# A four-layer graph network on one core: the first batch's adjacency transposed by TensorE, and the order tables written anew with another rule for the port that VectorE and GpSimd share

## The chip, the cores and the metric

One core of a Trainium2 chip runs the whole program. The core has five engines with an instruction queue each: TensorE (PE in the profile, with its weight loads as PEld), VectorE (DVE), ScalarE (ACT), GpSimd (POOL) and SyncE (SP). The metric is the device time of one execution in microseconds (us). The time of a kernel is the median of several executions. One more execution is recorded by the profiler, and its span runs from the first to the last instruction.

## The reference

There are 32 batches of 512 nodes with 128 features (x), and one 512 x 512 matrix of zeros and ones for each batch (adj, about 3% ones). Four layers follow each other, all of the form x + f(relu(layernorm(x)), adj):

```
layer 0:  p = h @ (W1 - W2);  q = h @ W2;  f[n] = max over m of relu(p[n] + q[m] + b) * adj[n, m]
layer 1:  four times: f = tanh([ norm(adj) @ src | self | norm(adj)^T @ dst ] @ wu + bu)
layer 2:  f = (adj / rowsum(adj)) @ (h @ w) + bias
layer 3:  four times a GRU cell on m = adj^T @ (h @ w3[l])
```

Both adj and its transpose are used in every batch. Layer 0 is a maximum over neighbours. It can't be one matrix product, and it is where most of the work on VectorE lies.

## The kernel before

The batches are independent, and the kernel works on several of them at a time. `batch(b)` is written once and has five parts. `load` fetches x and adj. `prepare` computes the normalised features, the transposed adjacency `at`, the products p and q (`pn`, `qn`, a table of q in memory), running counts of neighbours (`pc`, `cc`, `ccd`) and the indices of up to seven neighbours that are left over (`pkey`, `top`, `at8`, `idx`). `gathers` forms the maximum of layer 0 in two ways. For the first four neighbours of each column block, VectorE or ScalarE builds a selection matrix `oh` from `ccd`, TensorE multiplies it (`pa`), and VectorE takes the maximum into `acc`. The neighbours left over are fetched by GpSimd's indirect DMAs into `G`, and VectorE takes the maximum into `gm`. `layer1` and `layer23` do the rest; their products with the adjacency (`pg`) use each operand as a rounded part `hi` and a remainder `lo`. GpSimd computes `lo` with a subtraction in `sbuf_parts` (three times a batch), ScalarE computes `hi`.

In `prepare`, the transposed adjacency is made like this. ScalarE reads each of the four row blocks of the float32 matrix `af` and writes a bf16 copy `ab`, while it adds up the row sums. SyncE then issues four DMA transposes of 2-byte data from `ab` to `abt`. ScalarE copies `abt` to `at`, while it adds up the column sums. `ab` has two buffers and `abt` has one, which the next batch's `junk` also uses (a check that the matrix holds only zeros and ones).

**What sets the order.** Calls do not issue instructions. `Flow` records them with the buffers that they read and write, and then orders them. Every recorded operation has a due time in a table (`FRONT`, `MIDDLE`, `BACK`), and on every engine the operations stand in the order of these due times. `Flow.step` goes through the five queues with a simple model of the engines, in which every operation has a cost, and the model only decides in what order the queues take buffers and banks, and where TensorE is given `spin` matmuls (products of constants, into an unused bank, that keep it busy while it would wait). All instructions that go through `Flow` have one line in the profile, L1107; `spin` has L1133. `FRONT` has 12 rows: three for the weights and nine for batches 0 to 8. `MIDDLE` is one row, used for 13 batches, each shifted by `PERIOD`. `BACK` has ten rows, for batches 22 to 31. So from batch 9 to 21 the engines repeat one order.

**The port in the planner.** VectorE and GpSimd share a port to the on-chip memory. `Engine.note` marks the operations that take it (`port`): those with two large inputs in that memory, VectorE's `tensor_scalar`, and some on GpSimd. In `Flow.starts`, a marked operation of one engine starts only after the marked operation of the other. If GpSimd asks (`asked`) while VectorE holds the port and VectorE's next operation is marked too, the planner of this kernel lets VectorE go on: that is what `held` says.

Of the kernel before, what the change touches and what calls it, by code (L numbers as in the profile page):

```python
# [15 lines left out]
BF16 = mybir.dt.bfloat16  # L16
# [5 lines left out]
AX = mybir.AxisListType  # L22
# [20 lines left out]
    546.48,  # L43
    (
        "!!!!+b!+#!*D!*m!+u!4.!4?!4F!3o!Ab!KY!ZS![x!zp!|3!{=!{g!lw!^@!gV##n#(]#[`#_Z#_f#`C#dm!oU!"
        "v-#&f#)i#f%#fr#gc#hS#j6#n~#qX#th#oM#lm#pB#q{#tF#sb#u8#va#r*#ng#o9#pX#rV#ox#s7#p{#qI#x*$*"
        "7#u:$)V#qd#vg$#p#~r#wI$(v#sf#}R$%s$#3$!R#~5#m)#p|#rn$(~$8P$;:$=,#JN#x)#x7#}7#}>#~:$!%#x0"
        "#x>#yK#yQ#ym#zX#yX#{a#{}#|>#|c#}N#|i#})#}0$&k$,N$.P$/;$k^$/h$?n$A|$J_$1{$3A$6*$;[$0X$<B$"
        "4d$?[$7L$C2$9q$Io$?k$IF$A1$IZ$EX$Q1$JK$T>$Kn$U4$N2$Vn$Qj$^r$U($_*$VJ$_{$Wo$e<$_N$gX$aQ$k"
        "e$bt$ky$f%$ph$h5$p|$lA$u8$md%!v$qD$~9$t5%!M$uq$~M#{C#|P#~($$_$&`#|$$*Q$-/$,$$1O$!m$.=$3%"  # L50
        "$1w$45$)R$33$65$6Q$6}$4r$6j$8L$:l$>3$5S$;&$>{$?4$?q$:e$?K$A3$A.$D($@Q$DM$Dy$EN$Ez$BP$E}$"
        "G<$F~$H($CF$I.$Jg$MF$P;$FZ$N#$Rr$OS$S^$He$][$^5$]t$_>$TR$^:$b`$`~$cK$UH$a9$d7$bi$f2$a~$d"
        ";$j|$fT$l1$eQ$k=$nc$p~$sl$v0$y{$z1${0%#V%$G%%m%)K%(.%&k$RE%*9$`R%)=%(]$k$%Gq%H/%0e%0X%1b"
        "%-8%1M%4^%92%1v%5I%;l%<(%;s%=5%?=%=I%>?%=r%?x%Ao%OW%IR%KH%Mm%N2%NP%I^%J1%Jv%L&%L>%LU%Ll%"
        "MU%O0%Iv%JH%J_%KS%M&%Pa%Qx%S4%Sy%Q2%WA%X;%Y6%ZD%[=%[R%]$%]E%]e%^S%_R%`$%a=%aT%al%c>%cm%d"
        "(%dZ%`<%`k%a%%b>%bU%bm%c&%dV%eX%cU%dn%f8%g3%hA%i@%iK%iV%ix%j:%jy%kO%lh%m!%mQ%qH%qa%qx%rI"
        "%su%kh%l!%l9%mi%n;%nR%o$%r2%s8%n#%oS%pM%ra%t&%u6%v1%w?%xE%xP%y~%{V%{u%|W&$>&$U&&)&&@&(W&"
        "(o&)*&*+&,E&$m&%V&%n&&n&()&(@&)A&)X&-c&%?&03&3Q&5G&6q&7l&8f&9a&=s&Bl&Cz&Dy&E(&E2&E=&E]&H"
        "+&KY&H|&KE&LU&L]&MX&LN&N@&NX&O)&Of&Qe&Oz&RZ&R1&S5&TI&_M&YT&Z<&ZS&Zk&[%&[=&]&&]U&cr&eu&fY"
        "&gL&gn&iE&k^&hD&kx&j$&lg&mE&l{&l7&ml&me&m>&m~&n:&nK&oG&qO&pY&q&&o[&v;&w&&ts&u)&u4&uF&uf&"  # L60
        "vn&wt&xo&y*&yL&yd&y{&z6&zM&ze&{4&|2&}3&}@&~b(!S&{7&~.&~-(!Q(#>(#7($/(&1((-((8((C((N((m()"
        "O((Y()T(*N(*g(*~(+P(+h(+~(,9(,h(-7(.u(0B(0&(1P(2B(-!(27(1&(3F(42(5u(5#(6b(8F(9$(9:(9E(:?"
        "(;1(9P(:c(<X(>&(>>(>U(?&(?U(?m(@((@S(C4(AQ(DB(D~(F3(<p(D.(E/(F*(Fs(F{(Gd(HO(IN(IY(Ip(I{("
        "JX(KJ(J)(K#(K{(LM(L|(M7(Mf(M}(N8(NO(Nz(Ox(Ps(QU(Rt(Sf(N~(Qn(RB(S4(S}(TH(U)(Ur(Vz(W4(Wb(W"
        "m(Xl(Yg(XQ(Z$(ZK"
# [6 lines left out]
            "!!M!!!!*t!+,!*`!+8!+x!&r!0q"  # L72
# [13 lines left out]
        6.86,  # L86
        (
            "!%S!%&![B!jS!il!j=!i=!jr!!!!jq!ia!j2!n6!-:!j_!jH!j{!l+!ls!ml!m1!yV!vi!z<!zw!k>!ym!z&!y@!"
            "zP!{<!|w!zz#+`#,<#-z#.W!~)#,2#-o#,&#.1#.z#1>#/I#@M#@y#@c#C*#.y#@X#A(#@n#AG#B3#EU!#}#DB#F"
            "i"  # L90
# [5 lines left out]
            "!!!!$!!!O!)^!)5!)q!)I!*7!*0!*>!*)!*P!*i!*X!+v!-N!-%!,.!/m!1)!/-!09!;O!=H!.2!.G!.^!0O!0y!"  # L96
            "4G!6]!<R!>E!Fn!G_!HO!Iu!1p!4b!7e!5p!3g!2k!8*!8L!8W!9<!<0!=&!8W!Gn!IC!Jc!M&!J%!LF!H^!L*!W"
            "N!]L!Md![l!Jc!MO!Vn!V1!SR!Zq!Km!S@!X/!UP!Tp!T3!Jk!K0!N(!N;!NO!Nd!d5!>>!Ls!M(!Mn!N.!Ot!Q3"
            "!Mg!Mu!M|!N&!NA!O-!Q:!QH!QO!QV!Rg!T%!QA!Q^!Qe!Qk!R*!UT!V}!Zr!W7!Rx!Sq![Q!`H!c1!YO!ak!_%!"
            "e{!dU!hd!u=!j*!gA!qC!rf!|B!kL!w4!un!xX#%^!y{!~i!}F!|##+r##/#/r#.O#-,#8W#$Q#(T#+f#&2#9C!T"  # L100
            "m!Uh!V7!V#!W@!V@!W;!X-!WS!Xu!T%!W(!Ye!Z4!Y}!Z}!Y@!]!!^M!bs!^f!c_!eI!fE!fq!f]!g]!f+!g%!hH"
            "!il!j;!f+!gG!j&!k&!j>!ko!i9!jT!l!!l[!l:!qO!m^!qg!r;!rC!s(!n?!rZ!sp!s6!t[!np!u=!vh!x0!w!!"
            "yM!vY!wu!yC!zu!yb!{a!uz!yx!}!!z3!}k!wN!zJ#!,!{3##T!yX!zt!|B#$@!}z#&>!|f!~%#$3#(]#&C#*I#+"
            ">#+e#+p#+{#:b#<##>+#>J#=h#=I#>|!Wp!^&!]F!XP#3d#3~!gN#A6#A^#AJ#Ar#B*#B8#B1#B?#C(#De#EM#I*"
            "#M1#J1#I=#JZ#Ni#Q(#:q#Mq#M|#N*#N5#OB#O_#Rg#Rt#S0#S=#SI#Sb#So#UL#P%#RZ#S##SU#S{#T+#T7#TD#"
            "Ts#P3#TP#Ti#Tv#U%#U2#U?#UK#Uz#P?#T]#UW#Ud#Uq#U}#V-#V^#V}#VP#We#Vj#XA#W9#Wr#XT#Xm#Y<#Y|#Z"
            "##Z/#ZZ#Zf#ZM#Zx#[)#[|#[*#[W#[e#[q#[}#]`#]l#^A#_7#[=#].#]:#]R#]x#^(#^5#^Y#_X#[I#^M#^g#^s"
            "#_0#_<#_T#_b#`$#]F#_!#_H#_n#_z#`*#`7#`C#`d#`O#b&#`[#b:#a,#aW#b:#bg#c6#cu#cb#d(#dW#dc#dG#"
            "e3#eP#f6#d~#e|#f,#fE#g&#g?#h:#k=#k^#e5#eo#f8#f^#fj#fw#g3#gL#i9#eH#gX#gp#g}#h-#hF#hl#if#l"
            "E#fQ#hR#h_#i(#i4#iA#iM#iY#l##hx#kQ#is#ko#jB#l|#jn#n-#lP#o)#mL#nX#o<#oT#p##pc#q-#q8#qC#rR"  # L110
            "#q^#r+#rq#sb#r9#s*#s=#sb#tB#t[#u<#v7#x!#rE#sI#sU#so#s{#th#tt#un#y%#tN#u##uH#uU#ub#u{#v+#"
            "v]#z&#vC#vP#vi#vu#w%#wB#wO#wr#{E#x=#|p#xI#}{#xu#~c#yO$!2#y{$!^#zJ$#E#zv$#q#{^$$@#|-#|}#~"
            "_$$l$%R$&X$&i$&t$(8$([$)g$0K$//$/B$/V$1G$0`$3h$2|$5;$5S$5W$7{$8]$83$9R$9)$:-$<,$AC$:~$=j"
            "$>$$><$>S$>k$?%$@+$Bw$EW$F)$F?$FU$I?$Gt$IY$It$K8$KL$L]$Ka$M&$Lq$L|$LU$MA$MY$M:$Pi$Rj$Qt$"
            "P}$R@$S`$TX$TZ$Vi$W!$W.$W]$XS$YX$ZS$Zw$[2$[I$[x$]3$]J$]b$^0$_&$_~$`5$a0$b$$]y$aK$a!$bY$c"
            "F$cO$dD$eb$fa$gg$gr$g}$h?$i]$fl$hC$i>$jh$k#$k;$kR$kj$l#$l;$lg$me$pO$ns$q_$s2$lj$qJ$pt$sp"
            "$t]$v?$u_$w,$x.$x9$y>$yI$yh$zK$xC$yY${N${g$|9$|g$|~$}9$}P$~!$~N%%*%#G%&8%$U%([%!L%&R%(8%"
            ")3%)|%*(%*m%+v%,k%,v%-#%-/%-W%.c%-:%.M%/G%/`%/w%0I%0a%0w%12%1I%1u%2l%4y%46%6+%7/%1a%5t%6"
            "N%7@%8-%8e%9E%:c%;W%;c%<*%<4%<v%=N%=i%=4%>3"
# [3 lines left out]
        4.19,  # L123
        (
            "!!!!:U!0)!0Q!0=!/r!0x!0q!1*!1!!1<!1T!2O!2h!=f!=<!AG!;<!G{!Hu!LK!Tw!WY!T(!T3!T=!TH!Zg!LV!"
            "My!Uh!YF!ab!do!g|!if![^!^j!iU!`Y!]C!^>!aA!`{#$(##D#$w#&C!j&!cV!h`!q6!rS!qs!s4!en!i5!~D#("
            "Q!{v##B!lB!u@!|V!}7#!b#!$!lq#$i#16#0U#/@#.`!k.!p&!tQ!w<!wP!we!wx!XO!md!sS!sb!sw!ze!|%!sZ"
            "!si!sp!s~!u*!vG!zz!{,!{:!{H!~:#)L#&b#&i#&p#&w#(l#+`#+U#2Q#/G#(C#.&#.E#<v#><#?z#B<#08#EJ#"
            "2x#G(#5E#Hf#6o#LI#F4#Nc#IB#QQ#L=#TG#Ns#V}#P9#XZ#R.#Z<#U##^/#X-#a8#YQ#cR#Zu#dR#^g#fr#aq#i"
            "|#dF#lP#ei#n-#g[#of#jW#s=#m-#ub#nf#wB#pB#xM#sv#|v##8#(N#(z#(f#*u#*7#-O#-{#-g#.g#*p#,t#.B"  # L130
            "#/R#.e#0?#.7#/w#1E#1q#2X#3(#6>#79#8=#7Q#9*#7[#8W#9r#8o#;:#2F#4_#9*#<%#9A#<o#5{#8F#:##@*#"
            ":m#@r#>`#?[#BN#@-#C=#?H#A]#Dc#B/#FG#;%#>U#B^#G=#C0#H)#@9#B[#En#I$#F*#L^#D$#Fg#Nw#Le#Oc#E"
            "_#MX#PN#RR#T[#G@#It#V$#Xo#VR#Y[#L1#Mq#`*#`W#`S#ao#c~#g~#hX#j<#}l#~p$#<$$=$#z$#Z$%##1<#3|"
            "#9_#1y$$7$$Q#x0$&q$&^$&I$()$(=$(R$(D$(K$):$+`$)A$,m$-w$-#$.C$-M$.z$/f$*#$.Y$.e$/&$/1$/S$"
            "/o$1k$2U$2m$3>$4($4?$4V$5,$0B$2&$3U$3m$4n$5)$5@$5W$6%$0Y$0q$6A$7S$8b$9V$9b$9m$9x$:O$;2$;"
            "V$<s$=.$=E$>F$?/$?F$?^$@-$;n$<-$<[$=]$>]$>t$@p$AY$C<$>/$?u$C@$D=$EK$F@$FR$Fe$Fp$GO$H2$H@"
            "$Is$J]$MB$MZ$Mr$N-$O>$Ot$H_$I-$ID$I[$JE$Jt$L)$PQ$P}$J.$K.$LH$ND$OV$Q!$R,$S:$T;$TF$Ug$W)$"
            "WG$ZV$]6$^`$_2$`b$aK$ac$b5$bc$cW$^w$_I$_a$_x$`3$a4$az$bL$bw$`y$f*$jy$n_$oq$pl$q~$s4$vm$z"
# [2281 lines left out]
```

## Time and profile before

| | |
|---|---|
| time, three executions | 2809.97, 2811.62, 2818.3 us; median 2811.62 |
| profiled execution | 2811.83 us, span 2810.1 us |
| TensorE busy | 2715.8 us, 97% of the span |
| VectorE busy | 2450.8 us, 87% |
| GpSimd busy | 1687.4 us, 60% |
| ScalarE busy | 1263.9 us, 45% |
| mean granted TensorE clock | 0.993 |

The profiled execution is 0.2 us from the median, and 1.7 us longer than its span. A matmul counts as busy from its start until its modelled end, and the next one can start long before that, so 97% doesn't say that TensorE never waited. Times in the trace are counted from the start of the span. Two things give the pace. The store of a batch's result (`out_dram<-xo`, on ScalarE's queue) is the last instruction of a batch, so the distance of two stores is the time that one batch takes in the pipeline; the first is at 280.28 us and the last at 2799.9 us. The windows of the first 320 us show how the pipeline fills.

### The profile page before, as it was taken

Reading aid. Unit: us, or ns where it says so; the run is one execution under the profiler, and the core shown is the slowest. Engines: PE = TensorE matmul, PEld = TensorE weight load, DVE = VectorE, ACT = ScalarE, POOL = GpSimd, SP = SyncE. Lnnn points to the kernel's source line nnn. Section 1 sums busy time; section 2 is a strip of 40 time slices with the busy share of each in tenths; the row PEclk is TensorE's granted clock in tenths of the full one; section 3 lists DMA queues with packets and bytes.
Section 4 is the critical chain, followed back from the end, with each engine's and each line's share of the span. In section 5 each row is a group of like instructions: output and inputs, shape, how many; then the busy total and the mean of one; then the engine's idle time right before and its main releaser. Section 6 shows DMA issues by size and latency. Waiting matters only on the chain.

```text
span 2810.1 us, 36215 instructions
## 1 busy us (share of the span) xinstructions
PE 2715.8 (97%) x10690; PEld 1719.9 (61%) x10690; DVE 2450.8 (87%) x5739; ACT 1263.9 (45%) x2623; POOL 1687.4 (60%) x1892
## 2 busy tenths in 40 slices
PE   7799999999999999999999999999999999999997
PEld 4475666666666665666666666666666565656575
DVE  5888988899999998999999999999999898988544
ACT  5744444444444443444444444444444444443333
POOL 3766666666666666666666666666666666665410
PEclk9999999999999999999999999999999999999999
DMA  7754544344445444444444444454444454333200
GB/s 168 127 97 78 90 92 88 67 83 85 97 94 98 86 70 76 90 93 98 91 67 89 83 91 94 98 91 70 87 83 90 91 93 93 62 64 61 40 5 9
DMA packets 256752, 233.81 MB, mean 83 GB/s; under 512 B 98426, under 2 KB 205092, under 8 KB 256548
## 3 DMA queue, kind: packets, MB, share of 16 engines
q0 software_dynamic: 47104, 92.34, 24.4%
q1 hardware_dynamic: 143172, 81.41, 12.3%
q10 hardware_dynamic: 66272, 57.68, 6.9%
q8 instruction: 87, 1.43, 0.2%
q14 instruction: 117, 0.96, 0.1%
HBM read 163.79 MB, written 17.17 MB: 64 GB/s over the span
## 4 chain that ended last, share of the span: by engine, by line
PE 62%; DVE 21%; issue 7%; ACT 4%; POOL 4%; DMA 2%; SPq 0%; ACTq 0%; DVEq 0%; POOLq 0%
PE pg L1107 19%; PE pu L1107 13%; PE pk L1107 11%; DVE acc L1107 5%; PE pa L1107 4%; PE phn L1107 3%; DVE nn L1107 3%; PE pxn L1107 2%; DVE oh L1107 2%; DVE gm L1107 2%; PE ph L1107 2%; DVE h L1107 2%; ACT xn L1107 2%; DVE gate L1107 2%; PE pq L1107 1%
## 5 line engine op out<-in xcount | busy, mean ns | idle before, releaser
L1107 POOL DMA_INDIRECT G<-qtab,idx x744 | 786.5, 1057 | 530.3 <-DVE gm L1107 324.8
L1107 DVE TENSOR_TENSOR acc<-acc,pa 128x512 f32<-128x512 f32 x992 | 672.9, 678 | 43.2 <-PE pa L1107 14.0
L1107 PE MATMUL pa<-oh,qhl 128*128 128x512 f32 x1024 | 469.5, 488 | 18.6 <-DVE acc L1107 8.4
L1107 PE MATMUL pg<-an,hi 128*128 128x512 f32 (+1 forms) x1072 | 453.0, 429 | 0.2 <-ACT hi L1107 0.2
L1107 PE MATMUL pu<-ag,w 128*128 128x512 f32 (+1 forms) x952 | 440.8, 570 | 2.1 <-DVE ag L1107 2.1
L1107 PE MATMUL pg<-an,lo 128*128 128x512 f32 (+1 forms) x1072 | 411.6, 393 | 1.8 <-DVE lo L1107 1.0
L1107 DVE TENSOR_SCALAR oh<-ccd 128x1024 fp32r<-128x1024 bf16 x492 | 341.4, 705 | 3.1 <-PE pa L1107 2.9
L1107 ACT ACTIVATE xn<-x,shift,rstd 128x128 f32<-128x128 f32 x512 | 217.7, 485 | 233.4 <-POOL shift L1107 214.4
L1107 PE MATMUL pg<-at,hi 128*128 128x512 f32 (+1 forms) x672 | 284.1, 432 | 2.6 <-ACT hi L1107 1.9
L1107 PEld LDWEIGHTS pa<-oh,qhl 128*128 128x128 f32 x1024 | 191.5, 192 | 129.1 <-issue 57.6
L1107 PE MATMUL pg<-at,lo 128*128 128x512 f32 (+1 forms) x672 | 260.5, 396 | 0.6 <-POOL lo L1107 0.6
L1107 PEld LDWEIGHTS pu<-ag,w 128*128 128x128 f32 x952 | 174.3, 190 | 132.6 <-issue 100.1
L1107 PE MATMUL pk<-mT,g_ih 128*128 128x512 f32 (+1 forms) x528 | 254.5, 583 | 0.7 <-ACT mT L1107 0.7
L1107 PE MATMUL pk<-h,g_hh 128*128 128x512 f32 (+1 forms) x528 | 251.3, 582 | 0.9 <-ACT h L1107 0.7
L1107 PEld LDWEIGHTS pg<-an,hi 128*128 128x128 f32 x1072 | 201.8, 188 | 77.3 <-issue 22.8
L1107 ACT ACTIVATE gate<-pk,bsum 128x512 f32<-128x512 f32 (+1 forms) x264 | 173.0, 670 | 160.3 <-PE pk L1107 119.8
L1107 PEld LDWEIGHTS pg<-an,lo 128*128 128x128 f32 x1072 | 201.8, 188 | 69.9 <-issue 21.0
L1107 DVE TENSOR_TENSOR gm<-gm,G 128x128 f32<-128x128 f32 x744 | 232.8, 328 | 7.5 <-DMA G<-qtab,idx 6.5
L1107 ACT COPY mT<-pg 128x512 f32<-128x512 f32 (+1 forms) x164 | 93.9, 572 | 311.0 <-PE pg L1107 274.0
L1107 POOL TENSOR_TENSOR lo<-xn,hi 128x512 fp32r<-128x512 f32 x96 | 130.9, 1363 | 120.7 <-ACT hi L1107 116.4
L1107 POOL TENSOR_TENSOR rstd<-rstd,mhalf 128x4 f32<-128x4 f32 x128 | 139.9, 1093 | 102.1 <-DVE shift L1107 50.4
L1107 DVE TENSOR_TENSOR ag<-pg,rbc 128x512 f32<-128x512 f32 (+1 forms) x272 | 173.4, 650 | 20.6 <-PE pg L1107 18.9
(178 smaller groups left out, 5117.7 us busy)
## 6 DMA issues: line engine op xcount, KB each, us to landing
ccd<-cc SPq DMA_DIRECT2D x512, 64.0 KB
an<-in_adj_dram POOLq DMA_DIRECT2D x128, 256.0 KB
af<-in_adj_dram ACTq DMA_DIRECT2D x31, 1024.0 KB
rbc<-scal SPq DMA_DIRECT2D x32, 512.0 KB
x<-in_x_dram ACTq DMA_DIRECT2D x62, 256.0 KB
G<-qtab,idx POOLq DMA_INDIRECT x744
qtab<-qn SPq DMA_DIRECT2D x32, 256.0 KB
out_dram<-xo ACTq DMA_DIRECT2D x32, 256.0 KB
```

The source lines that it names most:

```text
L1107: op.fn(*(real(v) for v in op.args), **{k: real(v) for k, v in op.kw.items()})
```

## The change

There are three edits.

The first is in `prepare`, for batch 0 alone. The four DMA transposes and the buffer `abt` go. TensorE transposes the 16 blocks of 128 x 128 from `af` (float32) into four banks `pat`, and ScalarE copies these to `at` with the same instruction as before, which now reads a bank. The bf16 copies `ab` of batch 0 are still made, since their instruction adds up the row sums.

```diff
-        abt = F.tile(big, [P, NT, NT, P], BF16, tag="abt", name=f"abt_{b}")
-        for it in range(NT):
-            F.sync.dma_start_transpose(out=abt[:, it, :, :], in_=abs_[it])
+        if b:
+            abt = F.tile(big, [P, NT, NT, P], BF16, tag="abt", name=f"abt_{b}")
+            for it in range(NT):
+                F.sync.dma_start_transpose(out=abt[:, it, :, :], in_=abs_[it])
         for jt in range(NT):
+            if b:
+                v = abt[:, :, jt, :]
+            else:
+                v = pst(0, f"pat_{b}_{jt}")
+                for it in range(NT):
+                    F.tr(v[:, it, :], af[:, it, jt * P : (jt + 1) * P], W.ident, v)
             F.act.activation(
-                at[:, jt, :].rearrange("p (i q) -> p i q", q=P), abt[:, :, jt, :], AF.Identity,
+                at[:, jt, :].rearrange("p (i q) -> p i q", q=P), v, AF.Identity,
                 accum_out=deg[:, 1, jt : jt + 1],
             )
```

The second is the planner's rule for the port. When GpSimd asks between two marked operations of VectorE, or while the first of them runs, the port now goes to GpSimd at the end of that first one, and VectorE's next marked operation starts after GpSimd's.

```diff
                 asked = max(self.free["pool"] - self.HOLD, ops["pool"].ready)
-                held = self.port["vec"] > asked and self.port["vec"] > self.free["pool"]
-                if not held and asked < at["vec"] <= at["pool"] <= at["vec"] + self.HOLD + 1e-9:
-                    at["vec"] = at["pool"] + 1e-6
+                got = max(at["pool"], self.port["vec"])
+                if asked < at["vec"] <= got <= at["vec"] + self.HOLD + 1e-9:
+                    at["vec"] = got + 1e-6
```

The third is the tables: all of `FRONT`, `MIDDLE` and `BACK` have other due times. `FRONT` now has ten rows (batches 0 to 6), `BACK` nine (23 to 31), and `MIDDLE` serves the 16 batches 7 to 22. `PERIOD` and every cost of the planner stay. Every operation of a batch other than the first is the same as before; what differs is the order on all five engines, the buffers and banks that follow from it, and the number of `spin` matmuls (181 before, 165 after).

```diff
 MIDDLE = (
-    546.48,
+    369.07,
...
 FRONT = (
...
-    2161.25,
+    2233.47,
...
```

In a batch of the repeated order the instructions around GpSimd's subtraction `lo` of layer 1 stood like this before, and stand like this after (numbers of batches left out; both columns are orders, not times):

```
        VectorE                                            GpSimd
before  acc, lo(layer 3), oh, gm, oh, acc, acc, acc        gather, gather, lo, gather, rstd, has
after   oh, lo(layer 3), gm, oh, acc, acc, oh, acc         gather, an, has, lo, rstd, gather
```

In the first batch SyncE's queue before held the four transposes among the loads of the weights, ahead of the copies `ccd<-cc`. Afterwards these copies stand directly behind the loads of the bias rows, and the loads of `wn`, `wd` and `ws` of later weight groups stand among and behind them.

## The prediction

> **What bounds the kernel now.** I read the page's head first, then windows of one batch each in the repeated part, then the instructions of VectorE, GpSimd and the weight loads around the longest VectorE instruction in them, and last the first 50 us.
>
> ```profile
> span 2810.1 us, 36215 instructions
> ...
> PE 2715.8 (97%) x10690; PEld 1719.9 (61%) x10690; DVE 2450.8 (87%) x5739; ACT 1263.9 (45%) x2623; POOL 1687.4 (60%) x1892
> ...
> L1107 DVE TENSOR_TENSOR gm<-gm,G 128x128 f32<-128x128 f32 x744 | 232.8, 328 | 7.5 <-DMA G<-qtab,idx 6.5
> ```
>
> TensorE and VectorE are both close to full, so a wait on either can reach the other. The third line is odd. The groups by tile give the same 744 instructions as 247/282/1558 ns (shortest, median, longest). The mean of 328 is 46 ns above the median, 744 x 0.046 = 34 us in all: a few are very long.
>
> The windows from one store of a result to the next, and one such long instruction (VectorE, GpSimd, weight loads of TensorE; start, length, and in brackets the idle time before and what ended it):
>
> ```profile
> 1610.31:1692.29 81.98, 81.53 (x317) 51.62 (x315) 76.60 (x179) 37.23 (x78) 52.48 (x59) 1.00 0.46 88
> 1692.29:1774.25 81.96, 81.51 (x317) 51.60 (x315) 76.58 (x179) 37.21 (x78) 52.54 (x59) 1.00 0.45 88
> ```
> ```profile
> 1663.60 0.68 DVE L1107 TENSOR_SCALAR oh<-ccd 128x1024 fp32r<-128x1024 bf16 x1
> 1664.20 1.36 DVE L1107 TENSOR_TENSOR gm<-gm,G 128x128 f32<-128x128 f32 x1
> 1665.48 0.68 DVE L1107 TENSOR_SCALAR oh<-ccd 128x1024 fp32r<-128x1024 bf16 x1
> ...
> 1663.73 1.69 POOL L1107 TENSOR_TENSOR lo<-xn,hi 128x512 fp32r<-128x512 f32 x1 [0.42 <-issue]
> ...
> 1666.81 0.19 PEld L1107 LDWEIGHTS pa<-oh,qhl 128*128 128x128 f32 x1 [0.69 <-DVE acc L1107]
> ...
> 1676.54 0.20 PEld L1107 LDWEIGHTS ph<-ident,h 128*128 128x128 f32 x2 [0.54 <-DVE h L1107]
> ```
>
> A batch takes 81.97 us (DVE is the third busy column). In it GpSimd's `lo` starts at 1663.73, while VectorE runs `oh`. VectorE's next instruction, `gm`, takes 1.36 instead of 0.28, and ends when `lo` has ended; `lo` takes 1.69 where its median is 1.28. So the port went to GpSimd between two instructions of VectorE, and VectorE stood for 1.08 us. The planner of before says that VectorE goes on in this place. After it VectorE has no idle time until 1683, and TensorE waits for it twice.
>
> The start (the last line is the first selection matrix of layer 0):
>
> ```profile
> 11.29 2.28 DVE L1107 SCALAR_TENSOR_TENSOR junk<-af 128x2048 bf16<-128x2048 f32 x1
> ...
> 16.40 1.32 SPq L1107 DMA_TRANSPOSE abt<-ab  x1
> ...
> 23.28 1.20 SPq L1107 DMA_TRANSPOSE abt<-ab  x1
> ...
> 31.22 0.63 ACT L1107 ACTIVATE at<-abt 128x512 fp32r<-128x512 bf16 x1
> ...
> 34.94 0.64 ACT L1107 ACTIVATE at<-abt 128x512 fp32r<-128x512 bf16 x1
> ...
> 44.28 0.66 DVE L1107 TENSOR_SCALAR oh<-ccd 128x1024 fp32r<-128x1024 bf16 x1
> ```
>
> All of `af` is there at 11.29, since `junk` reads it whole, but the first piece of `at` is copied at 31.22. The 20 us between go to copies, two buffers `ab` that wait for each other, four transposes on SyncE's queue and their landing.
>
> **The change part by part.** *The regular stall.* Read one by one, `gm` takes 1.36 at one place in each of the 20 batches 7 to 26 (first at 591.7, last at 2156.7 us). In the new order `lo` is followed on VectorE by two `acc`, which read one operand from a bank and are unmarked; 2 x 0.68 covers the 1.28 of `lo`. If `lo` asks a little earlier, while `oh` runs, it gets the port at the end of `oh`, and still runs beside the two `acc`. So I cost the stall at nothing afterwards; if the cover fails, it is the same 1.08 again. Its worth on the path lies between the waits that TensorE shows behind it, over the 0.24 that a weight load often has from issue, (0.69 - 0.24) + (0.54 - 0.24) = 0.75, and the whole 1.08. I take 0.9, the middle: TensorE's row is the end of the path, but VectorE is full for 20 us after it. 20 x 0.9 = 18.0 us (15.0 to 21.6).
>
> *Eight irregular ones.* The same shows at 129.0 (1.28 lost), 331.7 (1.08), 2226.3 (1.57), 2269.5 (1.07), 2325.1 (1.27), 2354.8 (1.08), 2465.8 (1.62) and 2501.5 (1.10): 10.1 us. The new tables order these stretches too, by the rule that has GpSimd win. At the same ratio 0.9/1.08 that is 8.4 us (0 to 10.1). Another 82 waits of 0.12 to 0.6 us sum to 23.3; the new orders may shorten or lengthen them, so I take nothing, with half of it, 11.6, on each side as a bound.
>
> *The first batch.* Removed: four issues on SyncE's queue (1.32 + 1.19 + 1.19 + 1.20 = 4.9 us) and the landing behind the last one. Added: 16 transposes on TensorE. The nearest rows are the transposes `pt` of 128x128 float32, 0.27 alone and three in 0.52, so 0.125 apart: 2.0 to 4.3 us. They lie beside nothing of use: of TensorE's 26.66 busy us in the first 40, 15.27 are `spin`. ScalarE still makes four `ab` (0.62 + 0.19 each) and `hT` (0.56) first: 11.3 + 3.2 + 0.6 = 15.1 for the first copy to `at`, 16.1 us earlier than 31.22. The copy reads a bank now; the nearest row is `cc<-pc` with 0.58, against 0.63. The four banks `pat` take space that only `pt` and `pq` want then; should each wait for its predecessor's copy, that is 4 x 0.8 = 3.2 us. What is late next: `oh` came 13.1 us after the first copy, over `pc`, `cc` and the `ccd` copies on SyncE (0.6 each, 16 per batch). They now stand ahead of weights of layer 1. On SyncE the loads of `wn`, `wd`, `ws` behind them are later by up to 16 x 0.6 = 9.6 us; layer 1 needs them only after all of layer 0, whose first `gm` is finished past 108 us. On GpSimd the second batch's gathers and `rstd` come up with the tables; `junk` of batch 1, which waited 5.6 us for `abt`, is free of it. In the first 120 us TensorE is idle for 30 us and spins for another 35, so useful work moves with its data until the pipeline fills. Ends: 0, if weights or the second batch's data bind instead, and 16.1. I take 14, near the upper end, since the matrix feeds both branches of layer 0 and nothing else in these rows is late by as much.
>
> *A rule against this part.* The Trainium skill, TensorE: Matmul & The Clock Gate, Part 4: PE-mode transpose, gives about 275 ns for a transpose inside a kernel and says that transposes don't count as busy for the clock. By it the 16 take 4.4 us, 0.1 above my upper end, and replacing `spin` by them could cost clock. The rows before show a granted clock of 0.91 in the first 40 us, and no run yet shows transposes without `spin`.
>
> *The rest of the order.* The operations of batches 1 to 31 are the same, so no engine has less to do; TensorE's 81.5 busy us per batch limit any further gain.
>
> Sum: 18.0 + 8.4 + 14 = 40.4 us. The profiled execution took 2811.8 (span 2810.1), 0.2 above the median of the three, so both give 2771.
>
> **The rivals.** *The stalls move.* GpSimd has three `lo`, three sums and four `zc` per batch on the port. If the new order meets as many of them, only the front remains: 2811.8 - 14 = 2798. For it: all the repeated order is new. Against it: around `lo` of layer 1 the new order leaves two unmarked instructions.
>
> *The front is hidden.* If the first batch's layer 1 waits for weights anyway, only the stalls count: 2811.8 - 26.4 = 2785. For it: a load of `wn` issued at 22.66 kept TensorE waiting until 28.87. Against it: 65 of 120 us free.
>
> *Slower.* One mechanism: in the repeated part each batch has two long port waits where it had one, with one more `lo` or sum of GpSimd (1.28 each) between two marked VectorE instructions. It decides from 14/0.9, about 16 more long waits than the 28 of before. With 54, two in 27 batches, it is 26 x 0.9 = 23.4 more: 2811.8 - 14 + 23.4 = 2821. For it: VectorE is at 76.6 of 82 us, with little to absorb. Against it: the new rule makes such a place costly to the planner.
>
> *Nothing.* TensorE's 81.5 of 82 us may be real work; then neither VectorE's stall nor an earlier start is worth anything, and the time is 2812. Against it: TensorE's two waits behind the stall.
>
> **How the numbers follow.** Forecast 2771: 0.66, its own range 2757 to 2790. Stalls move, 2798: 0.12. Front hidden, 2785: 0.09. Nothing, 2812: 0.07. Slower, 2821: 0.06. The best ends together are 21.6 + 10.1 + 16.1 = 47.8, so 2764, and with half the small waits 2752; I start the range at 2753 and end it at 2799, just past the case of moved stalls, which leaves out 0.13 above and a little below. A change under 0.3% (8.4 us) can't be told from none in this kernel. Faster by more: 0.66 + 0.12 + 0.09 = 0.87; within: 0.07; slower: 0.06.
>
> **What would show it.** Right: the stores of two batches are 80.9 to 81.3 us apart instead of 81.97; the mean of `gm` falls to about 290 ns and its longest instances are rare; `at` of batch 0 is copied from about 15 us on, the first `oh` runs at about 30, and the first store comes 10 to 15 us before 280.28. Wrong: another group of VectorE has a mean well above its median, or `lo` above 1.28 for most of its 96; or TensorE at the start waits for loads of `wn` or `wd`, and the first store is where it was. One batch in the repeated part (stores at 1030.01 and 1114.59) took 84.6 us instead of 82.0; whatever that was could also come or go.

## The result: 0.5% faster, and the profile after

| | before | after |
|---|---|---|
| five executions each, median | 2818.24 us | 2800.90 us |
| lowest and highest | 2809.97 to 2818.53 | 2798.43 to 2801.37 |
| profiled execution (span) | 2811.83 (2810.1) | 2800.90 (2799.2) |

The ratio of the times is 0.9947, with a 95% interval from 0.9931 to 0.9963. The medians differ by 17.3 us and the profiled pair by 10.9, where the prediction had 40.4: the profiled execution of the kernel before is one of its faster ones, and all that follows from the two profiles accounts for the 10.9. The kernel became faster, but by much less than the forecast, and the time lies 2 us above the predicted range.

The store of a batch's result splits the profiled executions into four parts. The table gives their lengths in us, each worked out from the starts of two stores.

| | first store | 1st to 6th | 6th to 22nd | 22nd to last | last store |
|---|---|---|---|---|---|
| before | 280.3 | 421.5 | 1318.4 | 779.8 | 2799.9 |
| after | 283.7 | 414.2 | 1310.6 | 779.8 | 2788.4 |

So the fill of the pipeline (to the 6th store) is 3.8 us shorter, the repeated part 7.8, and the end not at all (a second profile of the changed kernel has 781.7 there). Within the fill the first store, which was to come 10 to 15 us before 280.28, comes 3.4 us after it. The page of the changed kernel (span; busy time of the engines; VectorE's maximum with the gathered rows):

```profile
span 2799.2 us, 36226 instructions
...
PE 2709.8 (97%) x10677; PEld 1721.8 (62%) x10690; DVE 2460.2 (88%) x5739; ACT 1284.0 (46%) x2623; POOL 1675.1 (60%) x1892
...
L1029 DVE TENSOR_TENSOR gm<-gm,G 128x128 f32<-128x128 f32 x744 | 245.6, 335 | 6.9 <-DMA G<-qtab,idx 6.1
```

The last line is the one to look at. The mean of `gm` is 335 ns, against 328 before. VectorE waits for the port as much as ever. Read one by one, 28 of VectorE's instructions took more than 0.6 us over the median of their kind before, 31.5 us in all; after, 49 did, 45.0 us in all. Of the smaller waits, 0.12 to 0.6 us, there were 82 with 23.3 us and are now 64 with 13.2.

The windows between two stores in the repeated part (the first number after the bounds is the time; DVE is the third busy column):

```profile
1599.38:1681.21 81.83, 81.52 (x317) 51.56 (x316) 76.93 (x179) 38.13 (x78) 52.13 (x59) 1.00 0.43 88
1681.21:1763.04 81.83, 81.49 (x316) 51.60 (x315) 76.90 (x179) 38.14 (x78) 52.70 (x59) 1.00 0.43 88
```

A batch takes 81.83 to 81.85 instead of 81.97 us. The old place of the stall is clean: beside GpSimd's `lo` of layer 1 VectorE now runs two `acc` and shows no wait.

```profile
1654.15 1.47 DVE L1029 TENSOR_TENSOR acc<-acc,pa 128x512 f32<-128x512 f32 x2
1654.31 1.28 POOL L1029 TENSOR_TENSOR lo<-xn,hi 128x512 fp32r<-128x512 f32 x1
```

Two other places in each of these batches have one. The first, in the timeline of the changed kernel (start, length, and in brackets the idle time before):

```profile
1671.41 0.68 DVE L1029 TENSOR_TENSOR ag<-pg,rbc 128x512 f32<-128x512 f32 x1
...
1671.90 1.27 POOL L1029 TENSOR_TENSOR lo<-xn,hi 128x512 fp32r<-128x512 f32 x1
1672.01 1.32 DVE L1029 TENSOR_TENSOR gm<-gm,G 128x128 f32<-128x128 f32 x1
...
1673.25 0.74 DVE L1029 SCALAR_TENSOR_TENSOR nn<-phn,bcol,gate 128x512 f32<-128x512 f32 x1
...
1676.70 0.69 DVE L1029 TENSOR_TENSOR h<-gate,nn 128x512 f32<-128x512 f32 x1
...
1677.51 0.14 PEld L1029 LDWEIGHTS ph<-ident,h 128*128 128x128 f32 x1 [0.62 <-ACT f L1029]
```

This `lo` is that of layer 2. It starts 0.11 us before `gm`, while VectorE runs `ag`, which takes one operand from a bank. So GpSimd has the port, and `gm` takes 1.32 instead of 0.28. The GRU's `nn` and `h` behind it are late, and so is TensorE's `ph`, which needs `h`: the profile puts this wait down to ScalarE's `f`, but `h` ended at 1677.39, just ahead of it. The second place:

```profile
1696.74 1.40 DVE L1029 TENSOR_TENSOR qhl<-qn,qhl 64x512 fp32r<-64x512 f32 x2
...
1697.58 0.63 POOL L1029 TENSOR_TENSOR shift<-shift,rstd 128x4 f32<-128x4 f32 x1
...
1702.58 1.27 POOL L1029 TENSOR_TENSOR lo<-xn,hi 128x512 fp32r<-128x512 f32 x1 [2.17 <-ACT hi L1029]
...
1703.05 0.96 DVE L1029 TENSOR_TENSOR gm<-gm,G 128x128 f32<-128x128 f32 x1
...
1703.62 0.20 PEld L1029 LDWEIGHTS pf<-ident,f 128*128 128x128 f32 x2 [0.44 <-ACT f L1029]
```

GpSimd's small `shift` falls into VectorE's second `qhl` and takes 0.63 instead of 0.20. ScalarE's `xn` waits for `shift`, and everything behind it on ScalarE is later: `hi`, so that `lo` of layer 3 meets a `gm`, and `f`, for which TensorE waits.

The start in the changed kernel:

```profile
12.88 0.60 ACT L1029 ACTIVATE at<-pat 128x512 fp32r<-128x512 f32 x1
...
15.89 1.24 ACT L1029 CAST cc<-pc 128x512 bf16<-128x512 f32 x2
...
22.25 1.16 SPq L1029 DMA_DIRECT2D ccd<-cc  x2
...
32.93 0.69 DVE L1029 TENSOR_SCALAR oh<-ccd 128x1024 fp32r<-128x1024 bf16 x1 [6.47 <-DMA ccd<-cc]
...
37.19 0.45 PE L1029 MATMUL pwt<-ident,ws 128*128 128x128 f32 x1 [6.05 <-DMA ws<-in_L_gnn_ws_dram]
```

The first copy to `at` comes at 12.88 instead of 31.22, the first `oh` at 32.93 instead of 44.28. Then TensorE stands for 6.05 us for the load of a layer 1 weight (`ws`, second group), with the first products `pa` behind it in its queue.

### The profile page after: what moved, and what is told of

Read it like the earlier page. It is cut to its first block, busy times and chain, and to the rows that moved or that the text cites. A ratio compares the mean times of both kernels' runs of the same rounds, so it can differ in the third digit from the quotient of the medians.

```text
span 2799.2 us, 36226 instructions
## 1 busy us (share of the span) xinstructions
PE 2709.8 (97%) x10677; PEld 1721.8 (62%) x10690; DVE 2460.2 (88%) x5739; ACT 1284.0 (46%) x2623; POOL 1675.1 (60%) x1892
## 3 DMA queue, kind: packets, MB, share of 16 engines
q1 hardware_dynamic: 140996, 80.88, 11.4%
## 4 chain that ended last, share of the span: by engine, by line
PE 78%; DVE 11%; issue 3%; POOL 3%; ACT 3%; DMA 2%; DVEq 0%; ACTq 0%; POOLq 0%; SPq 0%
PE pg L1029 24%; PE pu L1029 17%; PE pk L1029 14%; PE pa L1029 6%; PE phn L1029 3%; PE pxn L1029 3%; DVE nn L1029 3%; PE ph L1029 2%; DVE gm L1029 2%; PE pq L1029 2%; PE pf L1029 2%; DVE acc L1029 1%; DVE oh L1029 1%; DVE h L1029 1%; POOL G L1029 1%
## 5 line engine op out<-in xcount | busy, mean ns | idle before, releaser
L1029 PE MATMUL pa<-oh,qhl 128*128 128x512 f32 x1024 | 463.7, 488 | 10.9 <-ACT oh L1029 5.7
L1029 PE MATMUL pg<-an,hi 128*128 128x512 f32 (+1 forms) x1072 | 444.6, 421 | 0.0
L1029 PE MATMUL pg<-an,lo 128*128 128x512 f32 (+1 forms) x1072 | 426.5, 404 | 3.1 <-DVE lo L1029 2.3
L1029 PE MATMUL pg<-at,hi 128*128 128x512 f32 (+1 forms) x672 | 273.4, 416 | 0.7 <-ACT hi L1029 0.6
L1029 PE MATMUL pg<-at,lo 128*128 128x512 f32 (+1 forms) x672 | 268.0, 408 | 0.4 <-DVE lo L1029 0.2
L1029 DVE TENSOR_TENSOR gm<-gm,G 128x128 f32<-128x128 f32 x744 | 245.6, 335 | 6.9 <-DMA G<-qtab,idx 6.1
L1029 POOL TENSOR_TENSOR rstd<-rstd,mhalf 128x4 f32<-128x4 f32 x128 | 158.9, 1244 | 78.0 <-DVE rstd L1029 64.3
L1029 POOL TENSOR_SCALAR zc<-gate 128x512 f32<-128x512 f32 (+1 forms) x132 | 81.2, 615 | 173.9 <-ACT gate L1029 169.8
```

Source lines behind the costliest of these rows:

```text
L1029: op.fn(*(real(v) for v in op.args), **{k: real(v) for k, v in op.kw.items()})
```

## The experiments

Most of these kernels give some recorded operations other due times, just ahead of the ordering. `get` picks operations of one engine by the names of the tiles that they write or read, and `reorder` hands the same due times to the same operations in another order. Every run stood beside the kernel before on its own chip, and the ratios are to that.

### The old stall by itself

The kernel before, with five instructions of VectorE in another order in batches 4 to 26, and nothing else:

```diff
+                (f"lo_{b - 3}_3_1", f"hi_{b - 3}_3_1"), (f"oh_{b}_2_1", f"ccd_{b}_2"),
+                (f"gm_{b}", f"G_{b}_2_1"), (f"oh_{b}_2_2", f"ccd_{b}_2"),
+                (f"acc_{b}", f"pa_{b}_3_1_1"),
...
+                k = reorder([old[k] for k in (1, 0, 4, 2, 3)], 3.0); n += k
```

> The kernel before, with VectorE's order changed around the regular stall alone (batches 4 to 26): oh, lo of layer 3, acc, gm, oh instead of lo of layer 3, oh, gm, oh, acc, so that GpSimd's lo of layer 1 runs beside lo and acc, which take one operand from a bank. Everything else, the first batch's DMA transposes among it, is as before. Theory of the prediction (the stall costs 0.9 us a batch on the path, 18 us in all): gm of 1.36 us at this place is gone, stores stand 81.0 to 81.1 apart instead of 81.97, and the kernel takes 16 to 20 us less than the kernel before. Rival (the stall was worth little, as the changed kernel's 81.85 could also mean): 81.7 to 81.9 apart, 2 to 5 us less.

Measured: 2794.75 us against 2815.30 of the kernel before, ratio 0.9937 (0.9923 to 0.9951). The timeline of this kernel around `lo`, and a window from store to store:

```profile
1648.04 0.82 DVE L1107 TENSOR_SCALAR oh<-ccd 128x1024 fp32r<-128x1024 bf16 x1
1648.76 1.27 POOL L1107 TENSOR_TENSOR lo<-xn,hi 128x512 fp32r<-128x512 f32 x1 [0.42 <-ACT hi L1107]
1648.78 0.67 DVE L1107 TENSOR_TENSOR lo<-ph,hi 128x512 fp32r<-128x512 f32 x1
1649.38 0.67 DVE L1107 TENSOR_TENSOR acc<-acc,pa 128x512 f32<-128x512 f32 x1
1649.97 0.28 DVE L1107 TENSOR_TENSOR gm<-gm,G 128x128 f32<-128x128 f32 x1
```
```profile
1595.38:1676.28 80.90, 80.90 (x316) 51.83 (x315) 75.61 (x179) 37.21 (x78) 52.07 (x59) 1.00 0.44 89
```

GpSimd's `lo` takes 1.27 instead of 1.69, `gm` 0.28 instead of 1.36, and a batch 80.92 (mean from the 16th to the 22nd store) instead of 81.97. The stall was worth 1.05 us a batch, nearly its whole length of 1.08. These five moved instructions gain as much as the whole change that this document is about.

### The two new waits

One exchange of neighbours for the first wait (batches 7 to 27 and 30), and one `ag` between the two `qhl` for the second (batches 5 to 26); then both:

```diff
+            g = get("vec", f"gm_{b}", f"G_{b}_1_3")
+            m = get("vec", f"ag_{b - 1}_0", f"pg_{b - 1}_0_0_0")
...
+                n += reorder([g[0], m[0]], 0.75)
```

> One change to the changed kernel: in batches 7 to 27 and 30, VectorE's maximum gm with the gathered G (block 1, round 3) stands before the multiplication ag that it stood behind, so that GpSimd's lo of layer 2 runs beside ag, nn and acc, none of which showed a wait beside it. Theory (the wait of 1.03 us per batch at this gm is on TensorE's path, through nn and h of the GRU cell to the transposes ph, which come 0.41 later than in the order's own plan): the 1.32 us gm goes, the mean of gm falls from 335 to about 308 ns, stores stand 0.4 apart less, 81.45 instead of 81.85, and the kernel takes 2791 to 2793. Rival (TensorE's own work per batch sets the distance, or the second wait, 0.67 at gm with block 2 of round 6, takes up what is won): the mean falls as well, but stores stay 81.8 to 81.9 apart and the kernel takes 2799 to 2802.

```diff
+            old = sorted(get("vec", f"qhl_{b}"), key=lambda op: op.due)
+            for out, src in (
+                (f"gm_{b - 1}", f"G_{b - 1}_3_5"), (f"ag_{b - 2}_2", f"pg_{b - 2}_2_0_0"),
+                (f"acc_{b - 1}", f"pa_{b - 1}_4_3_1"), (f"ag_{b - 2}_2", f"pg_{b - 2}_2_1_0"),
+            ):
...
+                n += reorder([old[k] for k in (0, 5, 1, 2, 4, 3)], 4.0)
```

> One change to the changed kernel: in batches 5 to 26, VectorE's second multiplication ag of layer 1 (unit 2) stands between its two subtractions qhl, so that GpSimd's small shift of the last layer norm does not find the port taken twice in a row (it took 0.63 instead of 0.20 us). Theory (this 0.43 delays ScalarE's xn, its f and then TensorE's products pf by 0.33 per batch, and makes GpSimd's lo late, behind which gm waits 0.67): shift takes about 0.2, the wait of gm at block 2 of round 6 goes below 0.2, the mean of gm falls from 335 to about 317 ns, stores stand 81.5 apart and the kernel takes 2793 to 2795. Rival (what TensorE loses there it has to spare, or the other wait takes it up): gm's wait goes, stores stay 81.8 to 81.9 apart, and the kernel takes 2799 to 2802.

> The two changes of order together (gm before ag; ag between the two qhl). Theory (the two waits lie one behind the other on TensorE's path): both gains add up, stores stand about 81.1 apart, gm's mean is about 290 ns and the kernel takes 2784 to 2788. First rival (they lie on parallel branches that meet): the gain is that of the larger one, 81.4 and 2791 to 2793. Second rival (TensorE's own work sets the distance): 2799 to 2802.

| | stores apart (mean, 16th to 22nd) | mean of `gm`, ns | 6th to 22nd store | first store | time | ratio |
|---|---|---|---|---|---|---|
| changed kernel | 81.85 | 335 | 1310.6 | 283.7 | 2800.9 | 0.9947 |
| `gm` before `ag` | 81.45 | 308 | 1304.8 | 287.1 | 2798.2 | 0.9934 (0.9921 to 0.9948) |
| `ag` between the `qhl` | 81.68 | 321 | 1308.2 | 283.9 | 2801.9 | 0.9952 (0.9939 to 0.9966) |
| both | 81.27 | 297 | 1301.8 | 290.6 | 2795.6 | 0.9927 (0.9913 to 0.9940) |

The windows of the kernel with both, and from the one with `ag` between the `qhl` the place of `shift`:

```profile
1601.62:1682.88 81.26, 81.26 (x316) 51.66 (x315) 75.59 (x179) 38.38 (x78) 52.37 (x59) 1.00 0.44 88
```
```profile
1695.64 0.69 DVE L1029 TENSOR_TENSOR qhl<-qn,qhl 64x512 fp32r<-64x512 f32 x1
1696.35 0.69 DVE L1029 TENSOR_TENSOR ag<-pg,rbc 128x512 f32<-128x512 f32 x1
1696.49 0.20 POOL L1029 TENSOR_TENSOR shift<-shift,rstd 128x4 f32<-128x4 f32 x1
```

`shift` has its 0.20 again. The distance of the stores falls by 0.40, by 0.17, and by 0.58 with both, so the two waits lie one behind the other and both on TensorE's path: the rival that TensorE's own work sets 81.85 has fallen. The second wait is worth half of what was expected. The times do not show this gain in full. Each missed what its theory expected (2791 to 2793, 2793 to 2795, 2784 to 2788), and the 2801.9 of the second edit lies in the range of its rival. In these three profiles, all from one chip, the first store came up to 7 us later than in the changed kernel, with the same instructions up to there, and the changed kernel itself did not run on that chip. That is the next question.

### The start

The first edit undone alone, with the transposes by DMA placed ahead of the copies `ccd`, and the changed kernel beside it on the same chip:

```diff
-        if b:
+        if True:
             abt = F.tile(big, [P, NT, NT, P], BF16, tag="abt", name=f"abt_{b}")
...
+                due = due[:k] + [19.70, 19.71, 19.72, 19.73] + due[k + 4 : k + 20 : 5] + due[k + 20 :]
```

> The changed kernel with the first edit undone alone: the first batch's adjacency goes by four DMA transposes on SyncE's queue again, placed ahead of the copies ccd, so that the first copy to at comes at about 31 as in the kernel before (in the changed kernel at 15). Theory of the prediction (what is won at the first selection matrix is won at the end): the kernel takes 11 to 14 us more than the run of the changed kernel beside it. Theory after the result (TensorE's queue and later waits for weights, ScalarE's matrices and the clock hold the front in any case): 0 to 5 us more, with the 5th store 0 to 5 us later.

> The changed kernel once more, unchanged, to have it beside the other runs of this call. In the profiled executions so far, all with the same instructions up to 360 us, TensorE ran at half clock for 20.5 to 44 us of the first 130 us, and the first store came between 283.7 and 290.6. Theory (the front is a matter of when a wait falls into a stretch that decides on the clock, so that a load landing 0.2 us later costs several us): the front of this execution differs from the earlier one by some us again, in low-clock time and in the first store alike, while stores from the 6th to the 22nd stand 81.85 apart as before. Rival (the fronts of the other runs differed because of their edits): first store at 283.7 within 0.5, low-clock time 20 us.

The changed kernel took 2798.07 (ratio 0.9930, 0.9917 to 0.9944), the one with DMA transposes 2806.05 (0.9960, 0.9946 to 0.9974). TensorE's transposes are worth 8.0 us in this order: between the two theories. In the profiles the first store moves by 6.1 (283.1 to 289.2), and the later parts agree to 0.5. The first `at` and `oh` of the kernel with DMA transposes:

```profile
27.09 0.63 ACT L1029 ACTIVATE at<-abt 128x512 fp32r<-128x512 bf16 x1 [1.99 <-DMA abt<-ab]
```
```profile
40.20 0.69 DVE L1029 TENSOR_SCALAR oh<-ccd 128x1024 fp32r<-128x1024 bf16 x1
```

So 14.2 us at the first copy to `at`, between the two runs, are 7.0 at the first `oh` (33.2 to 40.2) and 8.0 at the end.

This run also shows the new tables without the first edit, with the transposes at the place chosen here. Its first store is 8.9 us later than the 280.3 of the kernel before, and its 1st to 6th store take 414.3 us instead of 421.5. So in the fill the new order starts later and then gains; TensorE's transposes give back 6.1 of the late start. Why the new order starts later is open. No run has the new port rule with the old tables, so what the rule does by itself isn't shown.

The changed kernel's second profile has its first store at 283.1 and half clock for 27.3 of the first 130 us (283.7 and 20.5 in the first profile): the clock moved and the store nearly stayed, against the theory stated for this run, if a little outside the 0.5 us of its rival.

Next the late weight load, by itself and with more `spin`, and the `spin` alone:

```diff
+        last = sorted(get("sync", "ccd_0_0"), key=lambda op: op.due)[3]
+        (ws1,) = get("sync", "ws1")
+        ws1.due = last.due + 0.01
```
```diff
-        n = int(0.7 * (gap - 0.4) / self.SPIN)
+        n = int(0.95 * (gap - 0.2) / self.SPIN)
```

> One change to the changed kernel: on SyncE's queue the load of the weight ws1 stands behind the fourth copy ccd of the first column block instead of behind the tenth copy, wn1 and wd1. Theory (TensorE's in-order queue stood 6.05 us at 37.19 for this load, with the first selection products behind it): the wait of the transposes pwt from ws goes from 6.05 to under 2, the first product pa comes at about 33.7 instead of 37.5, and if the front decides, the first store comes 3 to 4 us before its 283.73 and the whole kernel ends 3 to 4 us earlier, 2797. Rival (the next late thing takes over, as later waits of 2.9, 3.0 and 1.9 us before 160 us do not come from this load): the wait goes just the same, but the first store moves by less than 1 us and the kernel takes 2800 to 2801.

> The changed kernel with more spin: where TensorE is to wait in the order's plan, spin fills 95% of the planned wait instead of 70%. Theory (half clock in the first 130 us delays the front): low-clock time goes from 20 to 44 us down to under 15, the first store comes 3 to 6 us earlier than in the run of the changed kernel beside it, and the kernel is 3 to 6 us faster than that run. First rival (TensorE waits for data in the front, and a faster clock only makes it wait longer): low-clock time goes down as well, the time stays within 1.5 us. Second rival (spin that outlasts the wait holds up the work behind it): 1 to 4 us slower.

> The changed kernel with the longer spin (95% of the planned wait) and the earlier load of ws1 (behind the fourth copy ccd). The run with the longer spin alone had half clock for 6.8 us of the first 130 us and its first store at 280.6. Theory (the late load cost the front 3 to 4 us, and the run with the earlier load alone hid that behind 44 us of half clock): low-clock time stays under 15 us, the first store comes at 276 to 278, and the time is 2794 to 2796. Rival (other late things take over): first store 279.5 to 281.5, time 2797 to 2800.

The earlier load alone: 2805.69, ratio 0.9967 (0.9955 to 0.9979), so both expected times were missed. TensorE's wait fell from 6.05 to 1.78 (it is 2.03 in the changed kernel's second profile, so this number alone says little), and the first `pa` came at 34.3 instead of 37.5, but the first store at 286.9. The granted-clock records of that execution have half clock for 44 us of the first 130, against 20.5 in the first profile of the changed kernel. It also came from another chip, and has at 64.70 a wait of ScalarE of 8.84 us that is 2.40 in the changed kernel; the last section shows that this wait stands in every profile of the new order from that chip, whatever the edit. So this run alone settles nothing. The longer `spin` alone: 2798.14, ratio 0.9933 (0.9920 to 0.9947), the same as the changed kernel beside it (2798.07). One window from 10 to 130 us, of the changed kernel's second execution and of the one with more `spin` (the third number from the end is the granted clock):

```profile
10.00:130.00 120.00, 90.24 (x392) 51.44 (x389) 91.71 (x204) 82.21 (x174) 66.84 (x79) 0.89 0.78 142
```
```profile
10.00:130.00 120.00, 100.60 (x481) 56.11 (x480) 94.60 (x209) 85.08 (x178) 69.73 (x83) 0.97 0.80 144
```

The clock rises as expected and the time stays: the first rival. With both, 2795.97, ratio 0.9939 (0.9925 to 0.9953). That time is in the theory's range, but the ratio is no lower than that of the `spin` alone, and the first store came at 280.2, against 280.6 there, which is the rival's. So, beside the longer `spin`, the late load had cost TensorE a wait, but nothing measurable of the kernel's time.

Why an earlier start gains so little is best seen at the end of batch 0's layer 0, where GpSimd adds `pn` to `gm`. Before and after:

```profile
108.97 1.66 POOL L1107 TENSOR_TENSOR gm<-gm,pn 128x512 f32<-128x512 f32 x1 [1.89 <-DVE gm L1107]
```
```profile
92.27 1.26 POOL L1029 TENSOR_TENSOR gm<-gm,pn 128x512 f32<-128x512 f32 x1 [7.06 <-DVE gm L1029]
```

There the change is 16.7 us ahead, all that the prediction hoped for. But the windows of the planned instructions alone, without `spin` (first column: busy us and number of TensorE's matmuls), before and after:

```profile
0.00:40.00 40.00, 13.25 (x65) 8.45 (x65) 15.41 (x54) 18.30 (x61) 8.14 (x12) 0.91 0.59 160
40.00:92.00 52.00, 32.12 (x138) 19.21 (x138) 40.14 (x76) 35.12 (x64) 32.41 (x41) 0.84 0.90 148
92.00:160.00 68.00, 48.80 (x273) 37.87 (x274) 56.41 (x132) 45.88 (x85) 44.15 (x51) 0.97 0.71 134
```
```profile
0.00:40.00 40.00, 11.79 (x78) 9.70 (x78) 19.87 (x65) 19.81 (x57) 17.79 (x27) 0.92 0.77 189
40.00:92.00 52.00, 30.05 (x145) 20.30 (x145) 41.28 (x74) 32.83 (x63) 26.00 (x28) 0.90 0.96 119
92.00:160.00 68.00, 50.12 (x251) 35.90 (x250) 53.47 (x131) 48.57 (x90) 43.37 (x51) 0.95 0.67 135
```

By 160 us TensorE has issued 65 + 138 + 273 = 476 matmuls before, and 78 + 145 + 251 = 474 after, 16 of which are the new transposes: 458 without them, 18 fewer than before. Batch 0 was ahead, but TensorE, which is nearly full from then on, had no more behind it. The lead that the fill has in the end shows only later. By 280 us the counts are 923 before and 925 - 16 = 909 after; by 700 us they are 2492 and 2526 - 16 = 2510. These 18 more, at 0.23 us from one of the long products to the next, are 4.1 us, and the fill is 3.8 us shorter.

The run with DMA transposes has 893 by 280 us and 2481 by 700 us, the changed kernel beside it 929 - 16 = 913 and 2527 - 16 = 2511. That is 20 and 30 fewer, or 4.6 and 6.9 us, where the first store moved by 6.1 and the time by 8.0. So what counts at the end seems to be the work that TensorE gets done early, not how far batch 0 is. The counts fit this, but they do not prove it, and some matmuls can be missing from a trace.

### All edits together, and the last batches

> The two changes of order (gm before ag, ag between the two qhl) and the longer spin. Theory: stores from the 7th to the 22nd stand 81.27 apart as in the run with both changes of order, so 9 to 10 us less than the run of the changed kernel beside it, and a further 3 to 6 us if the longer spin shortens the front. Rival for the first (the gain in the repeated part is lost again in the last batches, as the 25th store came 89.3 after the 24th instead of 87.7): 5 to 8 us less. With the rivals for the spin: no further gain, or 1 to 4 us lost.

Both changes of order and the longer `spin`: 2789.61, ratio 0.9899 (0.9884 to 0.9914), 8.5 us less than the changed kernel beside it. That is a little under the 9 to 10 expected for the order. The 6th to the 22nd store take 1302.0 instead of 1310.8, so the gain is that of the order; the longer `spin` added nothing that can be seen.

> All four edits to the changed kernel: gm before ag, ag between the two qhl, the longer spin, the earlier load of ws1. Theory: stores 81.27 apart, as in the run without the earlier load (2789.6), and 3 to 4 us less than that, 2786. Rival (the load gains nothing): 2788 to 2791.

With the earlier load as well: 2785.72, ratio 0.9896 (0.9879 to 0.9913), which the ratios can't tell from the run before. In the end part of the changed kernel one `gm` is longer than all others. GpSimd's instructions beside it:

```profile
2417.90 1.26 POOL L1029 TENSOR_TENSOR lo<-xn,hi 128x512 fp32r<-128x512 f32 x1
2418.03 3.72 DVE L1029 TENSOR_TENSOR gm<-gm,G 128x128 f32<-128x128 f32 x1
2419.11 0.60 POOL L1029 DMA_DIRECT2D an<-in_adj_dram  x1
2419.73 1.29 POOL L1029 TENSOR_TENSOR x<-x,b 128x512 f32<-128x512 f32 x1
2420.97 0.63 POOL L1029 TENSOR_SCALAR zc<-gate 128x512 f32<-128x512 f32 x1
```

It was moved behind two `nn`, and the version with all four edits was run once more beside it:

```diff
+        (late,) = get("vec", "gm_29", "G_29_1_3")
+        (nxt,) = get("vec", "gm_29", "G_29_2_3")
+        late.due = nxt.due - 0.01
```

> The version with all four edits once more, to have it beside the next run. In both theories its time agrees with 2785.7 to within 3, gm with block 1 of round 3 of batch 29 takes 3.5 to 3.8 us again, behind three instructions of GpSimd (lo, x plus bias, zc) with the issue of a load among them, and the time from the 22nd store to the last is 776 to 779.

> All four edits, and in batch 29 alone VectorE's gm with block 1 of round 3 stands behind the two nn, where GpSimd's lo, x and zc are through. Theory (an irregular stall in the last batches is on the path like the regular ones, at 0.65 of its length, since TensorE's order came 2.4 late after it): the wait of 3.5 us goes, the time from the 22nd store to the last falls by 2 to 2.5, and the kernel is 2 to 3 us faster than the run beside it. Rival (the last batches are bound by something else, as 779.8 from the 22nd store on was the same before and after the change in spite of different stalls): that time stays within 0.7.

All four edits again: 2794.28, ratio 0.9920 (0.9907 to 0.9934); that is 8.6 more than the first time, on another chip, so the expected agreement was missed. Its later parts agree (414.0, 1301.8, 776.8), and the long `gm` has its 3.72 us again, but the first store came at 290.3 instead of 281.3. With the moved `gm`: 2791.22, ratio 0.9915 (0.9901 to 0.9929). The group of `gm` there, from 2380 to 2440 us (shortest, median and longest in ns):

```profile
L1029 DVE TENSOR_TENSOR gm<-gm,G x20: 275/282/407, 2390.9 to 2439.9; 128x128 f32<-128x128 f32 x20
```

From the 22nd store to the last it took 774.9 instead of 776.8. Of these 1.9 us, 1.7 lie at one place, between the 26th and the 27th store: 83.93 instead of 85.62, where every other run with the new tables has 85.3 to 86.1. So a wait of 3.4 us was worth 1.7 to 1.9 on the path, in one pair of profiles; a stall in the last batches does count.

## Why the prediction was wrong, and where it was right

**The regular stall, 18.0 us.** Its price was right, if a little low: 1.05 instead of 0.9 a batch, and the medians of the kernel before with and without it differ by 20.5 us. That the new order clears this place, with two `acc` beside `lo`, was right as well. The step that failed is "So I cost the stall at nothing afterwards". It looked at one of GpSimd's three `lo`, and at none of its small instructions. In the new order `lo` of layer 2 meets a `gm` (worth 0.40 a batch) and `shift` a `qhl` (0.17); together they took 0.58 back. Another 81.27 - 80.92 = 0.35 a batch separate the mended new order from the mended old one, and what these are is open. What is left of the term is 0.12 a batch.

**The repeated part gained 7.8 us for all that**, 1.9 by these 16 x 0.12. Most of the rest is the batches out of step that the prediction only mentioned: before, those with stores at 1114.6, 1198.1, 1362.8 and 1446.3 took 2.6, 1.5, 0.8 and 1.5 us more than 81.97; after, one took 1.1 more than 81.85. Three of them stay in the kernel before without its regular stall (2.4, 0.5 and 1.5). In the first of them before, and in the one after, a gather of GpSimd waits 3.1 us where it waits 0.5 in a batch in step (at 1103.55 before, 1097.89 after); then GpSimd's `zc`, VectorE's `gate` and TensorE's `ph` are late, `ph` by a wait of 2.38 and 1.32. What the gather waits for is open.

**Eight irregular stalls, 8.4 us.** Nothing came: 779.8 us from the 22nd store on in both. The new tables order these batches too, but, besides the regular ones, with seven waits over 0.6 us (8.2 us in all) where there were six (7.7). So the assumption that they go was wrong. The run with the moved `gm` has one wait there on the path at 1.9 of 3.4; for that one the ratio assumed, 0.9 of 1.08, was too high.

**The first batch, 14 us.** The first `at` came at 12.88, 2 us earlier than worked out. "`oh` came 13.1 us after the first copy" failed first: it came 20.0 after, since the first `ccd` stands behind six loads of bias rows on SyncE's queue, the first of them issued at 20.46, and was issued itself at 22.25, though `cc` was written from 15.89 on. From the first copy to that issue it is 9.4 us, against 3.9 before (31.22 to 35.07). That left 11.4 us. "So useful work moves with its data until the pipeline fills" failed next: batch 0 was 16.7 us ahead at 92 us, TensorE had issued no more work by 160, and the first store came 3.4 us later than before. Undoing the transposes costs 8.0 us, so the term for them was too large by 6; the new tables, which the prediction gave no cost in the start, reach the first store later, and the fill as a whole is 3.8 shorter in the profiled pair. The weights: layer 1 does need them late, but TensorE takes its queue in order, and the transposes of a weight (`pwt`, after a wait until 37.19) stood ahead of the first `pa` (37.50). Bringing that load forward had the first `pa` 3.2 us earlier, and gained nothing measurable.

**The sum.** Between the last stores of the two profiles lie 11.5 us. The 18.0 became 1.9, the 8.4 became 0, the 14 became 3.8 for the whole fill, and 5.9 came from what had no term, most of it the batches out of step.

**The rule weighed there.** The new transposes take 0.27 each, as the Trainium skill, TensorE: Matmul & The Clock Gate, Part 4: PE-mode transpose, has it, but ten in a row took 1.25 us, which is 0.11 from one to the next. The granted clock from 10 to 20 us, where all 16 lie beside other matmuls, was 1.00. No run here shows that they cost clock.

**The rivals.** "The stalls move", 2798, had the mechanism for the repeated part, with a chance of 0.12. That its number is also close is partly luck: it took 14 us from the start and nothing from the repeated part, where the profiled pair has 3.8 and 7.8. The argument against it, two unmarked instructions around one `lo`, was true of one place in three. Even the condition of the slower rival came true: two long waits a batch where there was one, 49 in all where it asked for 16 more than 28. They cost 0.58 a batch and not 2 x 0.9, as it had priced them.

## What to carry to other kernels

A stall between two engines on a shared port belongs to the order, not to the place: when an order is made anew, look at every instruction of the other engine that takes the port, and ask which instruction stands beside it if it comes 0.2 us earlier or later. One long wait, read in the timeline and moved aside by exchanging a few neighbours, can be worth as much as new tables, and its price can be measured alone. And a part that is ahead in the start need not be a gain at the end: compare how much work the engine that is full afterwards has done by then, not only when one batch passes a point.

## What was not expected of the hardware

**Who has the port.** `lo` started 0.11 us before `gm` and kept VectorE for 1.03 us. This agrees with the Trainium skill, SBUF — State Buffer, Who interferes with whom: the one that issues first has the port for its whole instruction. The page does not say who is next. In the 3.72 us of `gm` at 2418.03, VectorE waited through three instructions of GpSimd (`lo`, `x` and `zc`), although 0.6 us for the issue of a load lay between the first two. And a GpSimd instruction of 128 x 4 elements waited for the port too: `shift` 0.63 instead of 0.20.

**The start differs between executions of the same instructions.** With one start, the first store came at 281.3 on one chip and at 290.3 on another. In the slower one, ScalarE's copy of a weight product and TensorE behind it:

```profile
69.39 0.37 ACT L1029 COPY w<-pw 128x256 f32<-128x256 f32 x1 [12.36 <-remote]
```
```profile
69.82 1.22 PE L1029 MATMUL pa<-oh,qhl 128*128 128x512 f32 x2 [7.93 <-ACT w L1029]
```

In the faster one the same copy waited for 2.39 us:

```profile
58.46 0.37 ACT L1029 COPY w<-pw 128x256 f32<-128x256 f32 x1 [2.39 <-PE pw L1029]
```

From the first store to the 6th both took 414.0. TensorE had issued the products that the copy waits for by 61 us; why the copy did not run before 69 is open.

The profiles divide by chip. In all six of the new order from two of the chips this copy waited for 8.16 to 14.40 us (the earlier load alone, the three runs on the two new waits, and the last two runs). In the seven others, six from a third chip and one whose chip isn't on record, it waited for 2.39 or 2.40. The kernel before took no longer on those two chips (medians 2814.4 and 2815.8) than on the third (2817.5 and 2815.3), so the loss seems to belong to the new start. Only one kernel ran on both kinds of chip, so that the chip alone makes the difference is not shown. In a kernel whose later parts repeat to 0.3 us, this wait is worth up to 9 us, and two edits to the start can be compared only where both ran on one chip, as the longer `spin` and the DMA transposes did.
